# Routed expert tiles: rows turned by VectorE in 32-square pieces, first weights fetched per tile

## The chip, the cores and the metric

The kernel runs on one core of one Trainium2 chip. The metric is device time in microseconds (us) of one execution; lower is better. The engines of the core work from queues of their own: TensorE (PE, with its weight loads shown apart as PEld), VectorE (DVE), ScalarE (ACT), GpSimd (POOL) and SyncE (SP), which here only issues DMAs. A matmul on TensorE first loads a stationary operand[...] and then streams the moving operand past it; the sum lands in a PSUM bank of 512 fp32 columns.

## The reference

Everything is fp32. The input is x (2048 tokens by 256) and a context (1601 rows by 256). Four residual layers follow: a cross attention with 128 hidden columns, a mixture of experts, a two-way cross attention with a gate, and a small gated expert layer. The change is in the second one:

```python
def _ffn(x, w1, w2, w3):
    return jax.nn.silu(x @ w1.T) * (x @ w3.T) @ w2.T
shared = sum of _ffn over 2 shared experts, for every token
logits = xf @ router_w.T + expert_bias            # 8 routed experts
rw, sel = jax.lax.top_k(logits, 2)                # two experts for each token
rw = softmax(rw)
out = shared + sum over the two chosen experts of rw * _ffn(xf, w1[e], w2[e], w3[e])
```

An expert takes 256 columns to 512 hidden ones and back to 256.

## The kernel before

Tokens are held 128 to a tile, 16 tiles. The first attention (block 0) works in four blocks of 512 tokens. After it, `hT_f` has the normalised tokens turned (feature on the partition) and `h_f` has them as rows.

**Shared experts.** `hidden(e, b)` (L612) computes 512 tokens of the hidden layer of shared expert e: 16 fp32 matmuls with 512 moving columns, each of which shows as two instructions in the profile. `outward(e, b, act)` (L631) multiplies back and adds to the residual `xs`. Between the matmuls of the first two `hidden` calls stand the router's small matmuls (`route`, L605, one after each matmul).

**Routing.** From the router's result VectorE takes the best two experts (L647 to L682). Two small matmuls (L686) count the tokens of each expert that stand before a given one; from these VectorE computes the slot of each (token, choice) in a list sorted by expert, padded so that each tile of 128 slots belongs to one expert (L688 to L724): `owner[s]` is the expert of tile s, `used` the number of tiles. GpSimd then scatters the rows of `h_f` to the memory buffer `rows_in` by 32 indirect DMAs (L729), each of which waits for the one before. The rest of the shared experts' matmuls stand beside this on TensorE. Program order is: `hidden` for the first two blocks, `outward` for the first, first part of routing, `hidden` for the third, the counting matmuls, second part, scatters, and the remaining shared work.

**Routed tiles.** There are 39 possible tiles (`NSLOT`), and 36 of them (`NSURE`) are always run. `tiles(s0, s1, also)` (L841) is a software pipeline over them:

- `arrive(s)` (L792): one DMA on SP's queue brings 128 rows of 1 KB, two TensorE transposes turn them, VectorE copies the result to `rT`.
- `up(s, rT)` (L802): TensorE reads `owner[s]` into a register; `rT` is the stationary operand (128 tokens), the expert's first weights move with 512 columns, at an address from the register. Four matmuls, that is 8 instructions. Then silu on ScalarE and a product on VectorE give `act`, tokens on the partition.
- `turn(act)` (L817): four TensorE transposes and a ScalarE copy, to get `act` with the hidden index on the partition.
- `down(s, base, aT)` (L825): four matmuls (8 instructions) with 256 moving columns, a copy, and one indirect DMA on GpSimd's queue that scatters the rows to `rows_out`.

In round s of the loop TensorE does `up(s)`, `turn(s-1)`, the transposes of `arrive(s+2)`, `down(s-2)`. All three weights of all 8 experts lie in SBUF: L587 to L592 load them in 24 DMAs of 512 KB. `beside` (L856) issues the loads of the next layer in round 4 and reads `used` into a register on every engine in round 24. After the 36 tiles `ctx_rows("s", ks)` (L784) projects the context for the next layer (L231), and one branch on `used` (L867) runs tiles 36 to 38 or skips them; in this input it skips them.

The order on each engine's queue is made by a scheduler at build time, which may move an instruction past another that it does not depend on; `tc.issue_after` ties an order where it is used. SBUF is given out in pools; a load into a pool waits until the former user of the place is done, and everything behind it on SP's queue waits too.

Of the kernel before, what the change touches and what calls it, by code (L numbers as in the profile page):

```python
# [9 lines left out]
F32 = mybir.dt.float32  # L10
# [3 lines left out]
ALU = mybir.AluOpType  # L14
# [3 lines left out]
P = 128  # L18
S = 2048
SC = 1601  # L20
D = 256
DC = D // P
# [10 lines left out]
NE = 8  # L33
# [11 lines left out]
def xattn_ffn_kernel(ctx: ExitStack, tc: tile.TileContext, t: dict, out: bass.AP):  # L45
# [24 lines left out]

    def load_ctxT(pool, ends=(512, 1024, 1536, SC)):
        w = pool.tile([P, DC, SC], F32, name="ctxT")
        for lo, hi in zip((0,) + ends, ends):
            nc.sync.dma_start(w[:, :, lo:hi], t["ctxT"][:, :, lo:hi])
        return w

    rows_in = tc.dram_tile([NSLOT * P, D + 1], F32, name="rows_in")
    rows_out = tc.dram_tile([2 * S + P, D], F32, name="rows_out")  # L80

    rows_sub = tc.dram_tile([SC, 2 * D], F32, name="rows_sub")
# [31 lines left out]
    wk0 = load(cxp, "wk0", [P, DC, HID0], nc.scalar)  # L114
    ctxT = load_ctxT(cxp, (256, 512))
    load_x(0, nc.scalar)
# [25 lines left out]
    qkb = {n: load(raw, "b" + n, [P, DC]) for n in ("qc", "ks", "qs", "kc")}  # L142
    nc.sync.dma_start(wvs[:, :, 0:D], t["wvs"])

    make_identity(nc, ident)
# [187 lines left out]
    with ExitStack() as ph:  # L333
# [119 lines left out]
        for b in range(NB + 1):  # L453
# [3 lines left out]
            if b < NB:  # L457
# [3 lines left out]
                if last is not None:  # L461

                    add = sum_tiles(last[1], last[2], 0, NCT)
                    if b > 1:
                        tc.add_manual_dep(
                            add.ins, maxima[0].ins.name,
                            mybir.DependencyInfo(mybir.DependencyClass.Sync, mybir.DependencyReason.DATA),
                            reason="sums under the next maxima",
                        )
                    if b == 1:  # L470
                        with tc.issue_after(add.ins):
                            nc.gpsimd.memset(zero[:, 0:D], 0.0)
                            nc.gpsimd.iota(
                                zero[:, D : D + 1].bitcast(I32), pattern=[[0, 1]], base=2 * S, channel_multiplier=1
                            )
                        nc.sync.dma_start(
                            rows_in.rearrange("(n p) d -> p n d", p=P),
                            zero.unsqueeze(1).to_broadcast([P, NSLOT, D + 1]),
                        )
                acc = sp.tile([P, BW], F32, name="acc")  # L480

# [104 lines left out]
    rwp = sbuf(rx, "rwp")  # L586
    routed = []  # L587
    for n, src in enumerate(("ew1", "ew3", "ew2")):
        w = rwp.tile([P, NE, HID * DC], F32, name=f"r{src}")
        for e in range(NE):  # L590
            nc.sync.dma_start(w[:, e, :], t[src][NSH + e].rearrange("p c h -> p (c h)"))
        routed.append(w.rearrange("p e h -> p (e h)"))  # L592

    with ExitStack() as ph:
# [17 lines left out]
        def hidden(e, b):  # L612
            a1, a3, _ = experts[e]
            act = work.tile([P, NHC, BW], F32, name="act")
            for hc in range(NHC):
                cols = slice(hc * P, (hc + 1) * P)
                ps = [bank(ps_s) for _ in range(2)]
                for w, p in zip((a1, a3), ps):
                    for c in range(DC):
# [3 lines left out]
                        )  # L623
                        if routes:
                            routes.pop(0)()
# [5 lines left out]
        def outward(e, b, act):  # L631
            a2 = experts[e][2]
            for j in range(BT):
                i = b * BT + j
                y = bank(ps_m)[:, 0:D]
                for hc in range(NHC):
                    nc.tensor.matmul(  # L637
                        y, act[:, hc, j * P : (j + 1) * P], a2[:, hc, :], start=(hc == 0), stop=(hc == NHC - 1)
                    )
                nc.vector.tensor_tensor(xs[:, i, :], xs[:, i, :], y, ALU.add)  # L640

        shared = [(e, b) for e in range(NSH) for b in range(NB)]
        acts_of = {at: hidden(*at) for at in shared[:2]}
        outward(*shared[0], acts_of.pop(shared[0]))
        full = [P, NT, NE]
# [36 lines left out]
        nc.vector.tensor_tensor(both, hot[0], hot[1], ALU.add)  # L682
        acts_of[shared[2]] = hidden(*shared[2])
        at_ps = bank(ps_t)[:, : 2 * NE * NT].rearrange("p (k n) -> p k n", k=2)
# [57 lines left out]
        for n, at in enumerate(shared):  # L742
            if n > 1:
                if at not in acts_of:
                    acts_of[at] = hidden(*at)
                outward(*shared[n - 1], acts_of.pop(shared[n - 1]))
        outward(*shared[-1], acts_of.pop(shared[-1]))
    f0.close()
    ffw.close()


    l1 = ExitStack()
    l1k = sbuf(l1, "l1k", 1, "right")
    w1pool = sbuf(l1, "w1", 1, "right")
    w1 = {}
    raw1 = ExitStack()
    raw1p = sbuf(raw1, "raw1", 1, "right")
    bvs = []

    def second_layer_loads():  # L760
        bvs.append(load_row(l1k, "bvs", D))
        w1.update(
            ew=load(raw1p, "ew", [P, 2, DC, D]), ow=load(raw1p, "ow", [P, DC, D]), gw=load(raw1p, "gw", [P, DC, NE]),
            wv=load(raw1p, "wvc", [P, DC, D]), bg=load(raw1p, "bg", [P, DC]),
        )
        wg = t["wg"]
        w1["wg1"] = w1pool.tile([P, DC, D], F32, name="wg1")
        nc.sync.dma_start(w1["wg1"], wg[:, 0:DC, :])
        w1["wg2"] = raw1p.tile([P, DC, D], F32, name="wg2")
        nc.sync.dma_start(w1["wg2"], wg[:, DC : 2 * DC, :])  # L770
# [3 lines left out]
        w1["bv"] = load_row(raw1p, "bvc", D)  # L774
        return load_ctxT(raw1p)

    with ExitStack() as ph:
        work = sbuf(ph, "r0w", 3)
        in_tiled = rows_in.rearrange("(n p) d -> n p d", p=P)
        with nc.allow_non_contiguous_dma(reason="one element of each row"):  # L780
            nc.sync.dma_start(goes_to, rows_in.rearrange("(n p) d -> p n d", p=P)[:, :, D].bitcast(U32))


        def ctx_rows(n, r):  # L784
            project_T(
                ps_s, fold[n], ctxT, 0, SC,
                lambda o, cols, ps: nc.scalar.activation(
# [4 lines left out]
        def arrive(s):  # L792
            r = work.tile([P, D], F32, name="rin")
            nc.sync.dma_start(r, in_tiled[s][:, 0:D])
            tp = bank(ps_t)
            for c in range(DC):
                nc.tensor.transpose(tp[:, c * P : (c + 1) * P], r[:, c * P : (c + 1) * P], ident)
            rT = work.tile([P, DC, P], F32, name="rT")
            nc.vector.tensor_copy(rT.rearrange("p c q -> p (c q)"), tp[:, 0:D])
            return rT  # L800

        def up(s, rT):  # L802
            e = nc.tensor.value_load(owner[0:1, s : s + 1], min_val=0, max_val=NE - 1)
            base = nc.tensor.snap(e * (DC * HID))
            ps = [bank(ps_s) for _ in range(2)]
            for w, p in zip(routed, ps):
                for c in range(DC):
                    nc.tensor.matmul(  # L808
                        p, rT[:, c, :], w[:, bass.ds(base + c * HID, HID)], start=(c == 0), stop=(c == DC - 1)
                    )  # L810
            sl = work.tile([P, HID], F32, name="rsl")
            nc.scalar.activation(sl, ps[0], AF.Silu)  # L812
            act = work.tile([P, HID], F32, name="ract")
            nc.vector.tensor_tensor(act, sl, ps[1], ALU.mult)  # L814
            return base, act

        def turn(act):  # L817
            tp = bank(ps_t)
            for hc in range(NHC):
                nc.tensor.transpose(tp[:, hc * P : (hc + 1) * P], act[:, hc * P : (hc + 1) * P], ident)  # L820
            aT = work.tile([P, NHC, P], F32, name="raT")
            nc.scalar.copy(aT.rearrange("p c q -> p (c q)"), tp)
            return aT

        def down(s, base, aT):  # L825
            y = bank(ps_m)[:, 0:D]
            for hc in range(NHC):
                nc.tensor.matmul(  # L828
                    y, aT[:, hc, :], routed[2][:, bass.ds(base + hc * D, D)], start=(hc == 0), stop=(hc == NHC - 1)
                )  # L830
# [5 lines left out]
            )  # L836

        ks = l1k.tile([P, DC, SC], F32, name="ks")
        vs = l1k.tile([P, NCT, D + 1], F32, name="vs")
        kbs = l1k.tile([P, NCT], F32, name="kbs")  # L840
        def tiles(s0, s1, also):  # L841
            rT = {s: arrive(s) for s in range(s0, min(s0 + 2, s1))}
            hid, aTs = {}, {}
            for s in range(s0, s1 + 2):
                if s < s1:
                    hid[s] = up(s, rT.pop(s))
                if s0 <= s - 1 < s1:
                    base, act = hid[s - 1]
                    aTs[s - 1] = turn(act)
                if s + 2 < s1:  # L850
                    rT[s + 2] = arrive(s + 2)
                if s0 <= s - 2 < s1:
                    down(s - 2, hid.pop(s - 2)[0], aTs.pop(s - 2))
                also(s)

        def beside(s):  # L856
            nonlocal ctxT, count
            if s == 4:
                ctxT = second_layer_loads()
                nc.gpsimd.memset(vs[:, :, D : D + 1], 1.0)  # L860
            if s == 24:
                count = nc.values_load(used[0:1, 0:1], min_val=0, max_val=NSLOT)

        ctxT = count = None
        tiles(0, NSURE, beside)
        ctx_rows("s", ks)
        with tc.If(count > NSURE):  # L867
            tiles(NSURE, NSLOT, lambda s: None)
    rx.close()
# [429 lines left out]
```

## Time and profile before

| | us |
|---|---|
| median of 3 runs (lowest to highest) | 1075.43 (1075.1 to 1075.63) |
| the profiled execution's own time | 1075.38 |
| its span in the trace | 1073.6 |
| TensorE busy in the span | 1037.3 (97%) |
| routed tiles' matmuls: L808 / L828 | 131.2 / 68.0 |
| their transposes: L820 / L797 | 21.6 / 13.7 |
| granted TensorE clock, mean | 0.986 |

A group's row gives line, engine, operation, what is written and read, count, then busy time and the mean duration of one. Neighbouring matmuls overlap in the records[...], so the price of one in a stream is read from the distance of two starts, not from its duration. PEld rows are the weight loads that go with them. In a timeline or chain row the first number is the start, the second the length.

### The profile page before, as it was taken

What the parts mean: (1) busy time and instruction counts of PE and PEld (TensorE: products, weight loads), DVE (VectorE), ACT (ScalarE), POOL (GpSimd) and SP (SyncE); (2) the same over time, 40 slices, a digit from 0 to 9 for tenths busy, and PEclk for the clock granted to TensorE, in tenths of its full rate; (3) what the DMA queues carried; (4) which work ended last, traced back from release to release, by engine and by line L of the source; (5) the groups of instructions that cost most, each with busy time, mean ns of one, the idle gap of its engine ahead of it and who ended that gap; (6) DMA issues with size and microseconds to landing.
All of it is one profiled execution on the core that took longest, in us unless ns stands there. A gap on an engine that the chain in (4) does not pass through costs nothing.

```text
span 1073.6 us, 10976 instructions
## 1 busy us (share of the span) xinstructions
PE 1037.3 (97%) x3694; PEld 640.5 (60%) x3694; DVE 501.5 (47%) x1257; ACT 342.5 (32%) x569; POOL 234.5 (22%) x239
## 2 busy tenths in 40 slices
PE   7999999999999999999999999999999999999994
PEld 5644557655566566666665644464774476666872
DVE  4877785342222222222224745432504766676664
ACT  3765445111100112111114435322313633433321
POOL 2246450002232011111111007604044301110000
PEclk9999999999999999999999999999999999999996
DMA  9160004701113511111105000010004202110000
GB/s 318 61 159 0 1 1 159 312 5 40 35 49 58 158 45 45 47 48 45 40 26 162 6 1 0 1 40 20 20 20 141 80 1 60 40 49 10 11 10 20
DMA packets 42326, 62.81 MB, mean 59 GB/s; under 512 B 10461, under 2 KB 30045, under 8 KB 42270
## 3 DMA queue, kind: packets, MB, share of 16 engines
q1 hardware_dynamic: 35342, 43.73, 12.7%
q0 software_dynamic: 5824, 17.32, 5.1%
q10 hardware_dynamic: 1104, 1.05, 0.3%
q8 instruction: 31, 0.51, 0.2%
q14 instruction: 25, 0.20, 0.1%
HBM read 42.65 MB, written 19.44 MB: 58 GB/s over the span
## 4 chain that ended last, share of the span: by engine, by line
PE 84%; DVE 10%; ACT 2%; POOL 2%; issue 1%; DMA 1%; SPq 0%; DVEq 0%; ACTq 0%
PE sc L268 18%; PE sc L808 12%; PE sc L620 10%; PE mm L1022 8%; PE mm L828 6%; PE mm L637 5%; PE mm L327 4%; PE sc L231 3%; PE mm L518 2%; PE sc L1155 2%; PE sc L984 2%; DVE e L311 2%; PE tp L820 1%; POOL acc L448 1%; PE tp L1121 1%
## 5 line engine op out<-in xcount | busy, mean ns | idle before, releaser
L808 PE MATMUL sc<-rew,rT 128*128 x288 | 131.2, 599 | 0.8 <-DMA ew<-in_ew_dram 0.8
L620 PE MATMUL sc<-hT_f,ew 128*128 128x512 f32 x256 | 117.2, 600 | 0.0
L327 PE MATMUL mm<-vs,e 128*128 128x257 f32 (+1 forms) x416 | 96.4, 379 | 0.0
L311 DVE TENSOR_TENSOR e<-e,tp 128x2048 f32<-128x2048 f32 (+3 forms) x48 | 86.5, 1859 | 13.0 <-PE tp L303 13.0
L315 ACT ACTIVATE e<-e 128x2048 f32<-128x2048 f32 (+3 forms) x48 | 74.3, 1571 | 56.6 <-DVE e L311 56.1
L268 PE MATMUL sc<-hT,ks 128*128 128x512 f32 (+1 forms) x208 | 91.1, 592 | 0.0
L268 PE MATMUL sc<-qs,hT 128*128 128x512 f32 (+2 forms) x256 | 88.1, 500 | 0.9 <-ACT hT L963 0.9
L808 PEld LDWEIGHTS sc<-rew,rT 128*128 128x128 f32 x288 | 55.1, 192 | 55.5 <-issue 53.8
L1022 PE MATMUL mm<-e,hr 128*128 128x512 f32 (+2 forms) x256 | 88.0, 499 | 0.0
L270 ACT COPY e<-sc 128x512 f32<-128x512 f32 (+3 forms) x116 | 61.1, 535 | 81.0 <-PE sc L268 81.0
L276 DVE TENSOR_TENSOR m<-sc,m 128x512 f32<-128x512 f32 (+3 forms) x100 | 62.6, 626 | 51.5 <-ACT e L270 48.0
L327 PEld LDWEIGHTS mm<-vs,e 128*128 128x128 f32 (+1 forms) x416 | 77.2, 190 | 13.2 <-issue 2.8
L814 DVE TENSOR_TENSOR ract<-rsl,sc 128x512 f32<-128x512 f32 x36 | 24.8, 688 | 113.1 <-PE sc L808 113.1
L833 POOL DMA_INDIRECT rows_out<-rout,goes_to x36 | 35.0, 973 | 177.0 <-DVE rout L832 172.6
L620 PEld LDWEIGHTS sc<-hT_f,ew 128*128 128x128 f32 x256 | 46.4, 190 | 44.4 <-issue 44.0
L268 PEld LDWEIGHTS sc<-qs,hT 128*128 128x128 f32 x256 | 47.9, 189 | 37.2 <-issue 26.9
L1022 PEld LDWEIGHTS mm<-e,hr 128*128 128x128 f32 x256 | 48.2, 190 | 35.4 <-issue 28.2
L828 PE MATMUL mm<-rew,raT 128*128 x288 | 68.0, 379 | 0.0
L628 DVE TENSOR_TENSOR act<-sl,sc 128x512 f32<-128x512 f32 x32 | 22.0, 688 | 94.9 <-PE sc L620 91.7
L268 PEld LDWEIGHTS sc<-hT,ks 128*128 128x128 f32 (+1 forms) x208 | 38.3, 186 | 46.1 <-issue 44.0
L729 POOL DMA_INDIRECT rows_in<-h_f,slot x32 | 31.4, 982 | 143.4 <-DVE xs L640 75.0
L812 ACT ACTIVATE rsl<-sc 128x512 f32<-128x512 f32 x36 | 21.5, 597 | 125.8 <-PE sc L808 125.8
(267 smaller groups left out, 1466.8 us busy)
## 6 DMA issues: line engine op xcount, KB each, us to landing
rew<-in_ew_dram SPq DMA_DIRECT2D x24, 512.0 KB, 10.2
rows_in<-zero SPq DMA_DIRECT2D x1, 5011.5 KB, 20.7
rin<-rows_in SPq DMA_DIRECT2D x36, 128.0 KB, 2.1
g<-rows_out SPq DMA_DIRECT2D x8, 512.0 KB, 5.0
ew<-in_ew_dram SPq DMA_DIRECT2D x7, 512.0 KB, 5.5
rows_sub<-sgrow SPq DMA_DIRECT2D x12, 256.0 KB, 2.0
ctxT<-in_ctxT_dram SPq DMA_DIRECT2D x4, 512.0 KB, 7.1
out_dram<-xs SPq DMA_DIRECT2D x8, 256.0 KB, 2.1
```

The source lines that it names most:

```text
L268: nc.tensor.matmul(ps, kT[:, d, k * P : k * P + r], q[:, d, :], start=(d == 0), stop=(d == nd - 1))
L270: seen = [nc.scalar.copy(e[:r, k, :w], ps)]
L276: seen.append(nc.vector.tensor_tensor(m[:r, :w], ps, upto, ALU.max))
L311: nc.vector.tensor_tensor(part, part, bc[:r, :w].unsqueeze(1).to_broadcast([r, k1 - k0, w]), ALU.add)
L315: nc.scalar.activation(part, part, AF.Exp)
L327: nc.tensor.matmul(ov[:c, : D + 1], e[:r, k, j * P : j * P + c], v[:r, k, :], start=(k == 0), stop=(k == len(rows) - 1))
L620: nc.tensor.matmul(p, w[:, c, cols], hT[:, c, b * BW : (b + 1) * BW], start=(c == 0), stop=(c == DC - 1),)
L637: nc.tensor.matmul(y, act[:, hc, j * P : (j + 1) * P], a2[:, hc, :], start=(hc == 0), stop=(hc == NHC - 1))
L808: nc.tensor.matmul(p, rT[:, c, :], w[:, bass.ds(base + c * HID, HID)], start=(c == 0), stop=(c == DC - 1))
L828: nc.tensor.matmul(y, aT[:, hc, :], routed[2][:, bass.ds(base + hc * D, D)], start=(hc == 0), stop=(hc == NHC - 1))
L833: nc.gpsimd.indirect_dma_start(out=rows_out, out_offset=bass.IndirectOffsetOnAxis(ap=goes_to[:, s : s + 1], axis=0), in_=r, in_offset=None ...
L1022: nc.tensor.matmul(ov, hr[:, k, d * P : (d + 1) * P], e[:, k, :w], start=(k == 0), stop=(k == NT - 1))
```

## The change

- **A copy of the first weights in memory.** `first_w` is a new buffer of 8 x 1 MB. `reorder(e)` copies the two first weights of expert e into it with the feature index in another order, in 8 DMAs from memory to memory on SP's queue; 64 of them are issued during block 0, behind the clearing of `rows_in`. Only the last weight (`ew2`) of the routed experts is still loaded to SBUF as a whole.
- **Fetch per tile.** `fetch(s)` reads `owner[s]` on SP and brings that expert's 1 MB into one of three SBUF buffers.
- **Arrival by squares.** `arrive(s)` uses four DMAs with pieces of 256 bytes, and one VectorE transpose, which turns each 32 x 32 square by itself; the order of features that comes out is the one that `first_w` has. No TensorE transpose is left.
- **`up` with the operands changed round.** The weights are stationary (128 x 128), `rT` moves with 128 columns: 16 matmuls, 32 instructions. The result has the hidden index on the partition, so `turn` goes away and the product goes straight to `raT`. The loop is one stage shorter.
- **Routing earlier.** The router's matmuls all stand in the first `hidden` (one after each matmul, three in its second half); the first part of routing follows it, then the second `hidden`, the counting matmuls and the rest.
- **Start.** The fetches and arrivals of tiles 0 and 1 stand ahead of the last `outward`; the pools of the shared experts are closed after it.
- **Ties.** SP's fetches and arrivals, TensorE's register loads and VectorE's first turns are tied in order; the loads of the next layer go out one group a round from round 4 on.
- **Branches.** `ctx_rows` is cut in three pieces, and each of the tiles 36 to 38 has a branch of its own, one after each piece.

```diff
+    first_w = tc.dram_tile([NE, P, 2, DC, HID], F32, name="first_w")
+    def reorder(e):
+        for n, src in enumerate(("ew1", "ew3")):
+            for o in range(P // Q):
+                half = slice(o % DC * DC * Q, (o % DC + 1) * DC * Q)
+                nc.sync.dma_start(
+                    first_w[e, o * Q : (o + 1) * Q, n],
+                    t[src][NSH + e][half, o // DC, :].rearrange("(c q) h -> q c h", q=Q),
+                )
...
+                        for x in range(NE):
+                            reorder(x)
...
-    for n, src in enumerate(("ew1", "ew3", "ew2")):
-        w = rwp.tile([P, NE, HID * DC], F32, name=f"r{src}")
+    w = rwp.tile([P, NE, HID * DC], F32, name="rew2")
...
-                        if routes:
+                        for _ in range(min(len(routes), 3 if hc > 1 else 1)):
                             routes.pop(0)()
...
-        acts_of = {at: hidden(*at) for at in shared[:2]}
-        outward(*shared[0], acts_of.pop(shared[0]))
+        acts_of = {shared[0]: hidden(*shared[0])}
...
-        acts_of[shared[2]] = hidden(*shared[2])
+        acts_of[shared[1]] = hidden(*shared[1])
...
         def arrive(s):
-            r = work.tile([P, D], F32, name="rin")
-            nc.sync.dma_start(r, in_tiled[s][:, 0:D])
-            tp = bank(ps_t)
-            for c in range(DC):
-                nc.tensor.transpose(tp[:, c * P : (c + 1) * P], r[:, c * P : (c + 1) * P], ident)
+            r = work.tile([P, P // Q, DC, Q], F32, name="rin")
+            squares = in_tiled[s][:, 0:D].rearrange("(g a) (o w) -> o a g w", a=Q, o=P // Q)
+            for o in range(P // Q):
+                with behind("SP"):
+                    seen["SP"] = nc.sync.dma_start(r[o * Q : (o + 1) * Q].rearrange("a g c q -> a g (c q)"), squares[o])
             rT = work.tile([P, DC, P], F32, name="rT")
-            nc.vector.tensor_copy(rT.rearrange("p c q -> p (c q)"), tp[:, 0:D])
+            with behind("DVE"):
+                nc.vector.transpose(rT.rearrange("p c (g a) -> p g c a", a=Q), r)
...
+        def fetch(s):
+            w = wpool.tile([P, 2, DC, HID], F32, name="now")
+            with behind("SP"):
+                e = nc.sync.value_load(owner[0:1, s : s + 1], min_val=0, max_val=NE - 1)
+                e = nc.sync.snap(e)
+                seen["SP"] = nc.sync.dma_start(
+                    w.rearrange("p n c h -> p (n c h)"), first_w[bass.ds(e, 1)].rearrange("o p n c h -> p (o n c h)")
+                )
+            return w
...
-            for w, p in zip(routed, ps):
-                for c in range(DC):
-                    nc.tensor.matmul(
-                        p, rT[:, c, :], w[:, bass.ds(base + c * HID, HID)], start=(c == 0), stop=(c == DC - 1)
-                    )
+            for n, p in enumerate(ps):
+                for hc in range(NHC):
+                    for c in range(DC):
+                        mm = nc.tensor.matmul(
+                            p[:, hc * P : (hc + 1) * P], w[:, n, c, hc * P : (hc + 1) * P], rT[:, c, :],
+                            start=(c == 0), stop=(c == DC - 1),
+                        )
...
-        def turn(act):
...
+        def ahead(s):
+            fetched[s] = fetch(s)
+            rT[s] = arrive(s)
+
+        for s in range(2):
+            ahead(s)
+        outward(*shared[-1], acts_of.pop(shared[-1]))
...
+            for s in range(s0, s1 + 1):
                 if s < s1:
-                    hid[s] = up(s, rT.pop(s))
+                    hid[s] = up(s, rT.pop(s), fetched.pop(s))
+                if s + 2 < s1:
+                    ahead(s + 2)
                 if s0 <= s - 1 < s1:
-                    base, act = hid[s - 1]
-                    aTs[s - 1] = turn(act)
...
+                    down(s - 1, *hid.pop(s - 1))
                 also(s)
...
-        ctx_rows("s", ks)
-        with tc.If(count > NSURE):
-            tiles(NSURE, NSLOT, lambda s: None)
+        for n, s in enumerate(range(NSURE, NSLOT)):
+            ctx_rows("s", ks, n * 512, SC if s == NSLOT - 1 else (n + 1) * 512)
+            with tc.If(count > s):
+                tiles(s, s + 1, lambda s: None)
```

## The prediction

> **What bounds the kernel now.** I read the page first (shares, then the chain), then the chain around the routed tiles, then TensorE's timeline in one steady round and wherever short matmuls stand in a row, and last the DMA share of two stretches. From the page:
>
> ```profile
> PE 1037.3 (97%) x3694; PEld 640.5 (60%) x3694; DVE 501.5 (47%) x1257; ACT 342.5 (32%) x569; POOL 234.5 (22%) x239
> PE 84%; DVE 10%; ACT 2%; POOL 2%; issue 1%; DMA 1%; SPq 0%; DVEq 0%; ACTq 0%
> L808 PE MATMUL sc<-rew,rT 128*128 x288 | 131.2, 599 | 0.8 <-DMA ew<-in_ew_dram 0.8
> L820 PE MATMUL tp<-ident,ract 128*128 128x128 f32 x144 | 21.6, 273 | 0.0
> ```
>
> TensorE sets the time; in the routed tiles nearly nothing keeps it waiting (0.8 us ahead of L808, L820 never). So the change is priced by TensorE's stream there. The chain shows how the tiles begin, and two rounds:
>
> ```profile
> 334.01 8.65 PE mm L637 x40
> 342.65 1.31 SPq L68
> ...
> 346.17 4.85 DMA ew<-in_ew_dram
> ...
> 351.11 5.37 PE sc L808 x8
> ...
> 378.24 3.43 PE sc L808 x8
> 382.33 1.73 PE mm L828 x8
> 384.06 3.43 PE sc L808 x8
> ```
>
> L808 returns every 384.06 - 378.24 = 5.82 us. The first eight take 5.37 us in place of 3.43. The timeline of TensorE divides a round:
>
> ```profile
> 375.69 0.60 PE L820 MATMUL tp<-ident,ract 128*128 128x128 f32 x4
> 376.13 0.38 PE L797 MATMUL tp<-ident,rin 128*128 128x128 f32 x2
> 376.35 1.89 PE L828 MATMUL mm<-rew,raT 128*128 x8
> 378.07 3.60 PE L808 MATMUL sc<-rew,rT 128*128 x8
> 381.51 0.60 PE L820 MATMUL tp<-ident,ract 128*128 128x128 f32 x4
> ```
>
> By starts: four transposes 0.44, two 0.22, eight of L828 1.72, eight of L808 3.44 (0.430 each); sum 5.82, no gap. The shared experts' last matmul runs out at 347.8 (the timeline has L637 from 333.84 for 13.98) and the context projection begins at 561.9: 214.1 us for 36 tiles, of which 36 x 5.82 = 209.5 are rounds and 4.6 are the start (rows and pools late, then a first tile at about half pace).
>
> **The new `up`.** It has 32 pairs of weight load and matmul with 128 moving columns. Such pairs, real fp32 ones, stand in the trace:
>
> ```profile
> 230.20 0.38 PE L686 MATMUL tp<-both,before 128*128 128x128 f32 x2
> 230.42 0.39 PE L686 MATMUL tp<-both,ones 128*128 128x128 f32 x2
> 230.64 0.60 PE L637 MATMUL mm<-ew,act 128*128 128x256 f32 x2
> 572.18 0.86 PEld L231 LDWEIGHTS sc<-ctxT,fold_s 128*128 128x128 f32 x7 [0.24 <-issue]
> ```
>
> Starts of L686 are 0.22 us apart for two: 0.11 each. Seven weight loads in a row (65 moving columns) take 0.86, the last 0.19 long: (0.86 - 0.19) / 6 = 0.112. The weight load sets this pace[...]. The upper bound is the value projection of block 0 (L244, 18 pairs in a row, first start to last end 2.46 us, the last 0.27 long): (2.46 - 0.27) / 17 = 0.129. There the stream has two holes in which a PSUM bank is awaited; in `up` both banks were freed a round ago. I take 0.1117: 32 x 0.1117 = 3.57 us in place of 3.44.
>
> A rule speaks against it. The Trainium skill, "TensorE: Matmul & The Clock Gate", section "Back-to-back issue gap", gives sustained load-and-matmul pairs as about 81 ns with 128 columns and 131 ns with 512, a ratio of 0.62. Cutting 512 columns in four would then cost 4 x 0.62 = 2.5 times: `up` 8.5 us, a round 10.2, and the kernel some 155 us slower. This trace has 0.112 against 0.430, a ratio of 0.26. I use the trace.
>
> **The round after.** Six transposes go (-0.66), `up` gains 0.13, `down` keeps 1.73: 3.57 + 1.73 = 5.30 us, 36 x 5.30 = 190.8, a gain of 18.7. For this the other parts must stay under 5.30 us a tile:
> - VectorE: the old copy (0.42) becomes a transpose of 256 columns. The trace has none; between that 0.42 and the 0.69 of a 512-column product (L814). I take 0.5. VectorE was busy 43.4 of 174 us, 1.5 a tile; without that cover each 0.1 would be 3.6 us in all.
> - ScalarE loses a copy of 0.59. The product that `down(s-1)` needs is done about 1.1 us after `up(s-1)`, and `down(s-2)` (1.73) stands between, in the last round too.
> - TensorE's register load stays (0.30 us on its sequencer, which runs ahead); four address computations a tile go.
> - SP: a register load (0.30 on TensorE, 0.47 on SP at L862), about 0.2 of register work, five DMAs. These cost 0.32 (L794) to 0.43 (L62), and 1.0 when queues are full (24 loads in 23.89 us at L591). So 2.1 to 5.7 us; I take 2.8. The fetch of tile s+2 waits for `up(s-1)`; the four row DMAs and the next layer's loads wait behind it, and VectorE's turn for them, two rounds ahead of need.
> - DMA: each tile fetches 1.05 MB. The stretches:
>
> ```profile
> 176.00:206.00 30.00, 29.97 (x118) 16.93 (x117) 5.59 (x13) 6.90 (x13) 0.00 (x0) 1.00 0.99 388
> 376.00:550.00 174.00, 174.00 (x659) 109.15 (x658) 43.38 (x90) 35.50 (x60) 29.18 (x30) 1.00 0.14 44
> ```
>
> (The last two columns are the share of the 16 DMA engines and GB/s.) While weights streamed at 388 GB/s TensorE kept its pace. At that rate 1.05 MB takes 2.7 us; rows and scatters had 0.14 of 5.82 = 0.8 us, and 256-byte pieces can hardly double it (4,992 pieces of 4 bytes at L781 landed in 4.6 us). About 3.8 of 5.30 us. One 512 KB load on an empty queue landed in 4.2 us, so 1 MB takes about 5.6; the buffers give it two rounds, over 10. The scatter's landing (2.4 us, plus 0.97 issue) has 5.3.
>
> Against this stands the skill's "DMA: Bandwidth & Descriptors", table in section "Bandwidth": 1 MB alone is given 6.15 us. If fetches went one by one at that pace they would set the round: see the rivals. I take the 388 GB/s, from loads of the same kind.
>
> **The start.** Router matmuls: 64 pairs, 0.11 us each wherever they stand; moved, not saved. `hidden` of the first block then ends near 175.7 + 13.7 + 7.1 = 196.5 and the second near 210.2; the first part of routing (5.5 us on VectorE, with three residual adds in it) fits under it. The counting matmuls come at 210 in place of 230.2, the scatters end 20 us earlier, near 321 in place of 340.8. The last `outward` runs from 340.9 to 347.8 as now, so the rows, 1 MB and the turns of tiles 0 and 1 are there: the 4.6 us go. The cover is 20 us; when it is gone, the turns, which stand ahead of the last adds on VectorE, hold those up too.
>
> **Hidden parts.** The 64 copies go out on SP behind the clearing at 50.2, at 0.33 to 1.0 us each (21 to 64 us), with 8.4 MB read and written, about 67 us at the 125 GB/s that the clearing's stretch moved. SP has nothing else until 175.4, and the data is wanted at 320. Without that gap the 8 remaining weight loads would be late. Sixteen loads of 512 KB go from a stretch in which TensorE did not wait: nothing.
>
> **Branches.** Two more. At the present one TensorE waits 0.45 us and the first matmul is stretched: the last weight loads end at 573.0, the next matmul starts at 573.62. I take 0.7 each; between 0.45 and 1.3 (the chain's hole there). Cost 1.4.
>
> **Sum** against the profiled execution: -18.7 - 4.6 + 1.4 = -21.9: span 1073.6 to 1051.7, time 1075.38 to 1053.5. The median shown, 1075.43, differs by 0.05, so the same number stands for it.
>
> **Rivals.**
> 1. *The start stays* (the scatters do not end earlier, or something else on SP is late): 1053.5 + 4.6 = 1058. For: each scatter waits for the last one's landing, and fetches now share the DMA engines. Against: 20 us of slack.
> 2. *The pairs run at 0.129*: round 5.86, 36 x 5.86 = 211, gain 214.1 - 211 - 1.4 = 1.7, time 1074. For: the L244 row. Against: its holes are bank waits.
> 3. *The fetch sets the round, and it gets slower.* Place: SP's queue and the DMA engines in the tiles. With 1 MB in 6.15 us (170 GB/s), 1.05 + 0.13 MB are 6.9 us a tile, 36 x 6.9 = 249, time 1075.4 + 249 + 1.4 - 214.1 = 1112. It decides from (214.1 - 1.4) / 36 = 5.91 us a tile on, 200 GB/s; SP's upper bound of 5.7 comes near. Against: 388 GB/s, with nothing in flight but such loads.
>
> **How the numbers follow.** The sum as it stands 0.72 (own range 1049 to 1058: branches, a microsecond or two of changed order in later stages), rival 1 0.10, rival 2 0.07, rival 3 0.11. The range leaves out rivals 2 and 3 (0.18) and is 1047 to 1066, with room for a round of up to 5.5 us. What a measurement can tell from no change is about 0.2%, 2.2 us. Faster: 0.72 + 0.10 + half of rival 2 = 0.85; same 0.04; slower 0.11.
>
> **What will show it.** In the profile after: `up` starts every 5.30 us; 32 of its matmuls 0.112 apart; no PE tp rows in the tiles; fetches landing in under 7 us and never a releaser of `up`; no hole between L637 and the first `up`; three holes of 0.7 us at the branches. It is wrong if `up` shows idle time ended by DMA or VectorE, if pairs are further apart, or if a stage outside the tiles has moved.

## The result, and the profile after

The changed kernel takes 1107.84 us (1105.28 to 1108.18), the kernel before, measured beside it, 1076.02 us: a ratio of 1.0288, 95% interval 1.0272 to 1.0304. The prediction was 1053.5 us, about 22 us faster; what came is some 32 us slower. The span grew from 1073.6 to 1106.1 us.

Three parts of the page of the changed kernel (shares, TensorE's busy tenths in 40 slices, groups of instructions):

```profile
PE 1031.2 (93%) x4342; PEld 694.6 (63%) x4342; DVE 502.9 (45%) x1257; ACT 321.4 (29%) x533; POOL 235.7 (21%) x239
...
PE   7999999999999987788889999999999999999994
...
L840 PE MATMUL sc<-rT,now 128*128 128x128 f32 x1152 | 135.8, 276 | 16.4 <-issue 15.6
...
L855 PE MATMUL mm<-rew,raT 128*128 x288 | 70.9, 390 | 23.7 <-DVE raT L849 23.7
```

L840 is the new `up`, L855 is `down`. TensorE's busy time fell by 6 us and the span grew by 32, so the loss is waiting: 16.4 us ahead of `up` and 23.7 ahead of `down`, where the routed tiles before had 0.8 us ahead of their matmuls and 1.8 ahead of their transposes. The slices put it into one place, the 7s and 8s from 387 to 581 us, the tiles. (The chain of waits, from which the prediction started, is of no use here: on this trace it stops at a branch, at 606.60 us, and never reaches the tiles.)

TensorE's timeline of the changed kernel (start, length, what, count), first where the tiles begin, then in a later round:

```profile
334.94 13.98 PE L645 MATMUL mm<-ew,act 128*128 128x256 f32 x64
348.76 7.31 PE L840 MATMUL sc<-rT,now 128*128 128x128 f32 x64
355.90 1.89 PE L855 MATMUL mm<-rew,raT 128*128 x8
357.63 3.73 PE L840 MATMUL sc<-rT,now 128*128 128x128 f32 x32
361.20 1.89 PE L855 MATMUL mm<-rew,raT 128*128 x8
362.93 3.73 PE L840 MATMUL sc<-rT,now 128*128 128x128 f32 x32
```

```profile
447.44 3.81 PE L840 MATMUL sc<-rT,now 128*128 128x128 f32 x32 [0.92 <-issue]
452.10 1.99 PE L855 MATMUL mm<-rew,raT 128*128 x8 [0.85 <-DVE raT L849]
455.00 3.81 PE L840 MATMUL sc<-rT,now 128*128 128x128 f32 x32 [0.92 <-issue]
459.66 1.99 PE L855 MATMUL mm<-rew,raT 128*128 x8 [0.85 <-DVE raT L849]
461.49 3.73 PE L840 MATMUL sc<-rT,now 128*128 128x128 f32 x32
466.08 1.99 PE L855 MATMUL mm<-rew,raT 128*128 x8 [0.85 <-DVE raT L849]
468.99 1.24 PE L840 MATMUL sc<-rT,now 128*128 128x128 f32 x9 [0.92 <-issue]
```

The first fence is the prediction come true. The last shared matmul (L645, start 334.94 for 13.98) runs straight into the first `up`, with no hole; the round is 362.93 - 357.63 = 5.30 us; `up` takes 361.20 - 357.63 = 3.57, so its pairs are 0.1116 apart; `down` takes 1.73. It holds for the tiles 1 to 6. In the second fence the same work takes 455.00 - 447.44 = 7.56, then 461.49 - 455.00 = 6.49 and 468.99 - 461.49 = 7.50 us. `down` starts 4.6 us after `up` in place of 3.57 (1.02 to 1.09 of waiting for the product raT) in each of them. `up` starts 2.9 after `down` in place of 1.73 (about 1.18 of waiting) in every round up to tile 16, and in every other one after it. From tile 6 to tile 35 the mean round is (587.34 - 378.83) / 29 = 7.19 us. That is 29 x (7.19 - 5.30) = 54.8 us: the prediction missed the time by 1107.84 - 1053.5 = 54.3.

Which `down` stands there shows on VectorE, whose timeline in the same stretch of the changed kernel is:

```profile
454.13 0.42 DVE L859 COPY rout<-mm 128x256 f32<-128x256 f32 x1 [2.09 <-PE mm L855]
454.47 0.43 DVE L812 STREAM_TRANSPOSE rT<-rin 128x256 f32<-128x256 f32 x1
458.92 0.69 DVE L849 TENSOR_TENSOR raT<-rsl,sc 128x512 f32<-128x512 f32 x1 [4.02 <-PE sc L840]
459.53 0.44 DVE L812 STREAM_TRANSPOSE rT<-rin 128x256 f32<-128x256 f32 x1
461.69 0.42 DVE L859 COPY rout<-mm 128x256 f32<-128x256 f32 x1 [1.73 <-PE mm L855]
```

The product that the `down` at 459.66 waits for (L849, 458.92 for 0.69) is that of the `up` of 455.00. So up to tile 6 TensorE has `up(s+1)` between `up(s)` and `down(s)`; after it `down(s)` comes right behind `up(s)`, with nothing in between that could cover silu and product. And on VectorE the turn (L812, 454.47) that the next `up` (455.00) needs stands behind a copy of an output (L859, 454.13) that waits for `down`. The profile names nothing that ended most of these waits of `up` (`issue`); in one round, at 409.57, it names the turn (0.87 us), and in the one shown the turn ends at 454.90, 0.1 before `up` starts. Run 6 below tests the reading. The rows which that turn takes had been asked for 18 us earlier, at 436.6 (the four row DMAs of tile 16; in run 5 below such a DMA lands 5.1 us after its issue, the median between 376 and 400 us), so it was not late data that held it. Nothing in the kernel orders the turn against the copy, or `down(s)` against `up(s+1)`; the build has placed them so. The Trainium skill, "PSUM — Partial Sum Buffer", section "Engine vs sequencer instructions", calls VectorE's queue strictly first in, first out, and has TensorE's matmuls start in program order; the trace agrees: the turn, its data long asked for, starts within 0.4 us of the copy in front of it.

The last fence of the changed kernel answers the DMA share shown before (the columns are those of the windows there, the last two the DMA share and GB/s):

```profile
176.00:206.00 30.00, 29.96 (x129) 17.80 (x129) 10.67 (x73) 9.89 (x18) 0.00 (x0) 1.00 0.38 141
376.00:550.00 174.00, 141.22 (x993) 126.50 (x991) 36.27 (x74) 15.61 (x27) 25.47 (x28) 1.00 0.63 204
```

The first row is no longer the stream of weights at 388 GB/s, since sixteen of these loads went. In the second, the tiles, the DMA engines are busy 0.63 of the time, at 204 GB/s. That is near the 200 GB/s at which rival 3 (the fetch sets the round) begins to decide, and its forecast, 1112 us, is only 4 us from the measurement. Two stories, then: the order of two queues (theory A in what follows), or the fetched megabyte in one form or another (theory B). The first runs were chosen to part them.

### The profile page after: what moved, and what is told of

It is laid out like the page before. It is cut to its first block, busy times and chain, and to the rows that moved or that the text cites. A ratio compares the mean times of both kernels' runs of the same rounds, so it can differ in the third digit from the quotient of the medians.

```text
span 1106.1 us, 12495 instructions
## 1 busy us (share of the span) xinstructions
PE 1031.2 (93%) x4342; PEld 694.6 (63%) x4342; DVE 502.9 (45%) x1257; ACT 321.4 (29%) x533; POOL 235.7 (21%) x239
## 5 line engine op out<-in xcount | busy, mean ns | idle before, releaser
L840 PE MATMUL sc<-rT,now 128*128 128x128 f32 x1152 | 135.8, 276 | 16.4 <-issue 15.6
L840 PEld LDWEIGHTS sc<-rT,now 128*128 128x128 f32 x1152 | 132.6, 192 | 24.2 <-issue 21.9
L628 PE MATMUL sc<-hT_f,ew 128*128 128x512 f32 x256 | 114.1, 595 | 0.0
L855 PE MATMUL mm<-rew,raT 128*128 x288 | 70.9, 390 | 23.7 <-DVE raT L849 23.7
L335 PEld LDWEIGHTS mm<-vs,e 128*128 128x128 f32 (+1 forms) x416 | 77.5, 191 | 13.3 <-issue 2.8
L849 DVE TENSOR_TENSOR raT<-rsl,sc 128x512 f32<-128x512 f32 x36 | 24.7, 687 | 129.6 <-PE sc L840 129.6
L855 PEld LDWEIGHTS mm<-rew,raT 128*128 128x128 f32 x288 | 51.9, 190 | 35.5 <-DVE raT L849 29.9
```

The lines of the kernel that those rows point to most:

```text
L335: nc.tensor.matmul(ov[:c, : D + 1], e[:r, k, j * P : j * P + c], v[:r, k, :], start=(k == 0), stop=(k == len(rows) - 1))
L628: nc.tensor.matmul(p, w[:, c, cols], hT[:, c, b * BW : (b + 1) * BW], start=(c == 0), stop=(c == DC - 1),)
L840: mm = nc.tensor.matmul(p[:, hc * P : (hc + 1) * P], w[:, n, c, hc * P : (hc + 1) * P], rT[:, c, :], start=(c == 0), stop=(c == DC - 1),)
L849: nc.vector.tensor_tensor(aT.rearrange("p c q -> p (c q)"), sl, ps[1], ALU.mult)
L855: nc.tensor.matmul(y, aT[:, hc, :], second_w[:, bass.ds(base + hc * D, D)], start=(hc == 0), stop=(hc == NHC - 1))
```

## The experiments

All are measured against the kernel before on the same chip. It took 1079.29 us beside the first four and 1073.22 beside the last four, so between the two groups, and with the changed kernel, ratios and rounds compare better than times.

**1. A tie on TensorE.** `down` stays behind the latest `up` that was issued before it, which is `up(s+1)`:

```diff
+            seen["up"] = mm
...
             for hc in range(NHC):
+              with behind("up"):
                 nc.tensor.matmul(
                     y, aT[:, hc, :], second_w[:, bass.ds(base + hc * D, D)], start=(hc == 0), stop=(hc == NHC - 1)
```

> The changed kernel, with one more tie: each tile's last product (down of tile s-1) is queued on TensorE behind the last matmul of up of tile s. Nothing else. Theory A (order): the chip could always have run a round in 5.30 us, and lost 54 us because from tile 6 on the queue has down(s) directly behind up(s), so that TensorE waits for the product, and VectorE's turn of the next rows stands behind a copy that waits for down. With the tie every round is 5.30 us, the tiles take 36 x 5.30 = 191 us in place of 245, and the time is 1052 to 1056 us. Theory B (fetch): 1 MB a tile cannot come faster, the order only follows it. Then up waits for its weights instead, a round stays at 6.5 to 7 us and the time at 1095 to 1108 us.

Measured: 1085.82 us (1082.8 to 1088.76), ratio 1.0067 (1.0041 to 1.0092). Neither value came. A part of the loss went, and what was left had one shape in every round. The timeline of this kernel, TensorE and VectorE (L857 is `down`, L861 the copy of the output):

```profile
449.98 3.81 PE L840 MATMUL sc<-rT,now 128*128 128x128 f32 x32 [0.92 <-issue]
...
453.63 1.89 PE L857 MATMUL mm<-rew,raT 128*128 x8
...
455.56 0.43 DVE L861 COPY rout<-mm 128x256 f32<-128x256 f32 x1 [0.62 <-PE mm L857]
455.90 0.43 DVE L812 STREAM_TRANSPOSE rT<-rin 128x256 f32<-128x256 f32 x1
...
456.44 3.81 PE L840 MATMUL sc<-rT,now 128*128 128x128 f32 x32 [0.92 <-issue]
```

`down` now follows `up` without waiting. But the turn still stands behind the copy, the copy waits for `down`, and `up` waits for the turn: 456.44 - 453.63 = 2.81 from `down` to the next `up` in place of 1.73. The round is 6.46 us, 29 x 1.16 = 34 us in all. There are two orders that matter, not one: the expectation had named both, but took it that the tie on TensorE would put the second right too.

**2. Half the fetch.** Only the first of the two first weights is fetched, and used for both products; no tie:

```diff
-            w = wpool.tile([P, 2, DC, HID], F32, name="now")
+            w = wpool.tile([P, DC, HID], F32, name="now")
...
-                    w.rearrange("p n c h -> p (n c h)"), first_w[bass.ds(e, 1)].rearrange("o p n c h -> p (o n c h)")
+                    w.rearrange("p c h -> p (c h)"), first_w[bass.ds(e, 1), :, 0].rearrange("o p c h -> p (o c h)")
...
-                            p[:, hc * P : (hc + 1) * P], w[:, n, c, hc * P : (hc + 1) * P], rT[:, c, :],
+                            p[:, hc * P : (hc + 1) * P], w[:, c, hc * P : (hc + 1) * P], rT[:, c, :],
```

> The changed kernel with no further tie; only the first of the two first weights is fetched (512 KB a tile) and stands in for the second too, so the routed result is not the reference's. The build gives this kernel the program's order in the tiles (up(s), down(s-1)) to the end. Theory A: 1052 to 1056 us, as with the tie, because the order is right. Theory B: the same, because half the data is well under a round. It shows that the size of the fetch is what the build's order hangs on; the next kernel parts the theories.

Measured: 1057.29 us (1056.92 to 1067.05), ratio 0.9834 (0.9778 to 0.9889). Taken alone this would have made theory B look right: halve the transfer and the loss is gone. But another thing changed with it. With buffers of half the size the queues as built have `up(s+1)` ahead of `down(s)` through to the last tiles. Only from tile 12 to 14 does a part of `down(s)` come early, which costs 1.1 us in all; in the other rounds nothing waits in TensorE's timeline:

```profile
453.07 3.73 PE L840 MATMUL sc<-rT,now 128*128 128x128 f32 x32
456.64 1.89 PE L855 MATMUL mm<-rew,raT 128*128 x8
458.37 3.73 PE L840 MATMUL sc<-rT,now 128*128 128x128 f32 x32
```

So the run doesn't part the two by itself, and the next one was needed.

**3. Half the fetch, in the changed kernel's order.** As 2, with `down(s)` put right behind `up(s)` from tile 6 on in the program, and each later `up` tied behind the `down` before it:

```diff
+                      with behind("down" if s >= 7 else "none"):
...
-                nc.tensor.matmul(
+                seen["down"] = nc.tensor.matmul(
...
+                late = s >= 7 and s0 <= s - 1 < s1
+                if late:
+                    down(s - 1, *hid.pop(s - 1))
                 if s < s1:
                     hid[s] = up(s, rT.pop(s), fetched.pop(s))
...
-                if s0 <= s - 1 < s1:
+                if not late and s0 <= s - 1 < s1:
                     down(s - 1, *hid.pop(s - 1))
```

> As half_fetch (512 KB a tile, the second first weight left out), but from tile 6 on TensorE is given the changed kernel's order: down(s) directly behind up(s), up(s+1) behind it. VectorE turns the rows of the next tile ahead of the copy that follows down. Theory A: TensorE waits about 1.1 us a round for the product, a round is 6.4 us from tile 7 on (29 rounds), time about 1054 + 29 x 1.1 = 1086 us. Theory B: with half the data nothing waits, 1052 to 1057 us.

Measured: 1084.34 us, ratio 1.0055 (1.0035 to 1.0076). TensorE's timeline (L841 is `up`, L856 `down`) has the wait for the product back, and a round of 391.00 - 384.58 = 6.42 us:

```profile
384.58 3.73 PE L841 MATMUL sc<-rT,now 128*128 128x128 f32 x32
389.17 1.99 PE L856 MATMUL mm<-rew,raT 128*128 x8 [0.85 <-DVE raT L850]
391.00 3.73 PE L841 MATMUL sc<-rT,now 128*128 128x128 f32 x32
```

With the same half megabyte the order on TensorE alone costs 27 us. The fetch can't be charged with that.

**4. Twice the fetch.** Both ties (the second is that of run 5), and a second megabyte a tile into two buffers that nobody reads:

```diff
+            more = morepool.tile([P, 2, DC, HID], F32, name="more")
+            with behind("SP"):
+                seen["SP"] = nc.sync.dma_start(
+                    more.rearrange("p n c h -> p (n c h)"), first_w[bass.ds(e, 1)].rearrange("o p n c h -> p (o n c h)")
+                )
```

> The kernel with the tie, and each tile fetches a second megabyte that nobody reads; VectorE's copy after down is tied behind the turn of the rows two tiles on. It measures the room on the DMA engines. In the changed kernel a tile keeps the 16 engines busy for about 4.05 us (0.58 of a mean round of 6.97). Theory A: a second megabyte adds 2.7 to 3.2 us, about 7 us, over the 5.30 of TensorE: a round of about 7 us, time 1054 + 36 x 1.7 = 1110 to 1120 us. Theory B (1 MB already needs 6.5 to 7 us): two need 11 to 13 us, time 1260 to 1330 us.

Measured: 1103.98 us, ratio 1.0238 (1.0201 to 1.0275). Its window, and a turn on VectorE:

```profile
400.00:560.00 160.00, 135.43 (x952) 123.38 (x951) 34.08 (x71) 14.81 (x25) 22.28 (x24) 0.97 1.03 363
...
493.03 0.45 DVE L813 STREAM_TRANSPOSE rT<-rin 128x256 f32<-128x256 f32 x1 [1.28 <-DMA rin<-rows_in]
```

Here DMA is the bound: a share of 1.03 at 363 GB/s, the turn that `up` needs waits for its rows to land, the mean round is (583.99 - 385.49) / 29 = 6.84 us, and the time is somewhat under what either theory gave. Three of these rounds hold an `up` of 5.27 to 6.75 us in place of 3.81, in stretches where the granted clock fell to 0.87 to 0.89; from tile 17 on, without such, the round is 6.45. So two megabytes and the rows (2.10 + 0.13 MB) need 6.5 to 6.8 us, and one (1.18 MB) an estimated 3.4 to 3.6 at the same rate. The prediction's 3.8 us of DMA per tile was about right, and one megabyte has room in a round of 5.30.

**5. Both ties.** Experiment 1's tie, and on VectorE the copy of an output behind the turn of the tile two ahead:

```diff
-                nc.vector.transpose(rT.rearrange("p c (g a) -> p g c a", a=Q), r)
+                seen["turn", s] = nc.vector.transpose(rT.rearrange("p c (g a) -> p g c a", a=Q), r)
...
-            nc.vector.tensor_copy(r, y)
+            with behind(("turn", s + 2)):
+                nc.vector.tensor_copy(r, y)
```

> The changed kernel with two ties more, nothing left out: the matmuls of down(s) stay behind the last matmul of up(s) in TensorE's queue (which, as the tiles go, puts them behind up(s+1) for every s), and VectorE's copy of a tile's output, rout(s), stays behind the turn of s+2. Theory A (the whole error of the prediction is the order in two queues): the round is 5.30 us in all 36 tiles, no hole ahead of up, and the kernel takes what the prediction's sum said with the branch as predicted, 1052 to 1056 us, some 20 to 25 us below the kernel before. Theory B (with fetches of a megabyte the round has another floor, DMA or the load on SBUF, that half the fetch hid): the round stays above 5.8 us and the kernel above 1070 us, with DMA busy over 0.85 of the stretch.

Measured: 1054.51 us (1054.3 to 1054.86), ratio 0.9823 (0.9809 to 0.9836). All of the change is in it, with the full fetch; only the order of two queues differs from the changed kernel, and it is 53 us faster than that (by the ratios 4.6%, some 50 us). Page, a window (the same columns as above), and both engines in one round:

```profile
PE 1016.9 (97%) x4342; PEld 691.9 (66%) x4342; DVE 502.5 (48%) x1257; ACT 321.2 (31%) x533; POOL 235.6 (22%) x239
...
L840 PE MATMUL sc<-rT,now 128*128 128x128 f32 x1152 | 134.3, 275 | 0.0
...
L857 PE MATMUL mm<-rew,raT 128*128 x288 | 68.0, 379 | 0.0
```

```profile
400.00:560.00 160.00, 159.10 (x1102) 143.16 (x1101) 45.84 (x104) 22.26 (x37) 29.28 (x32) 1.00 0.69 229
```

```profile
453.93 3.73 PE L840 MATMUL sc<-rT,now 128*128 128x128 f32 x32
457.50 1.89 PE L857 MATMUL mm<-rew,raT 128*128 x8
457.77 0.69 DVE L850 TENSOR_TENSOR raT<-rsl,sc 128x512 f32<-128x512 f32 x1 [3.22 <-PE sc L840]
458.37 0.44 DVE L812 STREAM_TRANSPOSE rT<-rin 128x256 f32<-128x256 f32 x1
459.23 3.73 PE L840 MATMUL sc<-rT,now 128*128 128x128 f32 x32
459.43 0.42 DVE L862 COPY rout<-mm 128x256 f32<-128x256 f32 x1 [0.61 <-PE mm L857]
```

Idle time of 0.0 ahead of both groups, a round of 459.23 - 453.93 = 5.30 us, and the DMA engines carry more per microsecond than in the slow kernel (229 against 195 GB/s in the same window), because the rounds are shorter. VectorE's turn (458.37) now comes ahead of the copy (459.43), a round early. A fetch lands 5.2 us after its issue. Theory B had 1070 us and over.

**6. The tie on VectorE alone.** Run 5's second edit, without run 1's:

```diff
+            with behind(("turn", s + 2)):
+                nc.vector.tensor_copy(r, y)
```

> The changed kernel with VectorE's tie alone: rout(s) behind the turn of s+2, TensorE's queue as the program builder leaves it, so that from tile 6 on down(s) stands directly behind up(s). Theory A (two orders, each with its own price): up(s+1) no longer waits for a turn, but TensorE waits for silu and product of its own tile, the 0.85 to 1.04 us of the changed kernel's rounds, in every round: about 6.3 to 6.4 us from tile 6 on, some 1053 + 29 x 1.05 = 1083 us (1080 to 1088). Theory B (either tie is enough, since one chain runs through both): 1052 to 1060 us. Theory C (VectorE's order was only a consequence of TensorE's): as the changed kernel, 1100 to 1110 us.

Measured: 1086.36 us, ratio 1.0119 (1.0103 to 1.0134). In its timeline `up` follows `down` without a wait and `down` waits for its own product in each round of 461.57 - 455.15 = 6.42 us:

```profile
455.15 1.99 PE L855 MATMUL mm<-rew,raT 128*128 x8 [1.20 <-DVE raT L849]
456.98 3.73 PE L840 MATMUL sc<-rT,now 128*128 128x128 f32 x32
461.57 1.99 PE L855 MATMUL mm<-rew,raT 128*128 x8 [0.85 <-DVE raT L849]
```

With 1, 5 and 6 the two orders have a price each:

| | time, us (ratio) | round, us, tiles 12 to 35 | `down` waits for its product | `up` waits for a turn |
|---|---|---|---|---|
| changed kernel | 1107.84 (1.0288) | 7.07 | each round | each, from tile 16 every other |
| tie on TensorE | 1085.82 (1.0067) | 6.45 | no | each round |
| tie on VectorE | 1086.36 (1.0119) | 6.43 | each round | no |
| both | 1054.51 (0.9823) | 5.31 | no | no |

The last column but one and the last are read from the idle time noted in the timelines. The rounds add up. The late turn alone costs 6.45 - 5.30 = 1.15 us a round and the late product alone 6.42 - 5.30 = 1.12; where the changed kernel has both in one round it takes 7.56, which is 2.26 over 5.30, against 2.27 for the sum of the two. From tile 16 on two of its rounds hold twice the wait of `down` (1.09 and 1.02 over its 3.57), once the late turn (1.18 over 1.73) and once 0.10 of a stretched `down`: (1.09 + 1.02 + 1.18 + 0.10) / 2 = 1.70 us a round, and 7.00 is the mean of the 6.49 and 7.50 shown. With one tie only one wait is left, but in every round.

**7. One branch in place of three.** As 5, with the table loads in one piece and tiles 36 to 38 under one branch:

```diff
-        for n, s in enumerate(range(NSURE, NSLOT)):
-            ctx_rows("s", ks, n * 512, SC if s == NSLOT - 1 else (n + 1) * 512)
-            with tc.If(count > s):
-                tiles(s, s + 1, lambda s: None)
-            seen.clear()
+        ctx_rows("s", ks)
+        with tc.If(count > NSURE):
+            tiles(NSURE, NSLOT, lambda s: None)
+        seen.clear()
```

> Both ties, and the last three tiles under one branch again with one set of table loads, as in the kernel before. The prediction priced two branches more at 0.7 us each. If a branch that isn't taken costs what the holes of the changed kernel's end show (0.54 us each), this one is about 1.1 us below the kernel with both ties; if the holes are hidden by the scatters behind, the two are within 0.3 us.

Measured: 1053.12 us (1050.83 to 1053.67), ratio 0.9806 (0.9793 to 0.9819): 1.4 us less than with three, though the intervals of the two ratios overlap. It has the lowest median of the study, 20 us below the kernel before. The context projection (L239) with three branches and the first matmul behind it (L969), in TensorE's timeline of run 5, and the same two ends with one branch, in that of run 7:

```profile
540.45 3.60 PE L239 MATMUL sc<-ctxT,fold_s 128*128 128x512 f32 x8
544.35 2.81 PE L239 MATMUL sc<-ctxT,fold_s 128*128 128x512 f32 x6 [0.30 <-PEq L917]
547.46 5.37 PE L239 MATMUL sc<-ctxT,fold_s 128*128 128x512 f32 x18 [0.30 <-PEq L917]
...
575.69 1.89 PE L969 MATMUL mm<-wg,vT 128*128 128x256 f32 x8
```

```profile
540.23 11.30 PE L239 MATMUL sc<-ctxT,fold_s 128*128 128x512 f32 x32
...
574.61 1.89 PE L968 MATMUL mm<-wg,vT 128*128 128x256 f32 x8
```

The idle time noted is 0.30 us, but the price is more. Six L239 matmuls at 0.43 are 2.58, and from one hole to the next there are 547.46 - 544.35 = 3.11: 0.53 a branch. The whole stretch, with the same matmuls in it, takes 575.69 - 540.45 = 35.24 us with three branches and 574.61 - 540.23 = 34.38 with one: two more cost 0.86 us there. The rest of the difference between the two times stands elsewhere in the traces and is not explained.

**8. Five buffers.** The changed kernel with more room for fetches:

```diff
-        wpool = sbuf(ph, "r0x", 3)
+        wpool = sbuf(ph, "r0x", 5)
```

> The changed kernel with five buffers for the fetched weights instead of three and no tie more. In the order as built the down that comes directly behind its own up appears at tile 12 instead of tile 6. Theory A (order sets the time): six rounds more of about 5.3 us instead of 7.0 us, about 10 us below the changed kernel: 1096 to 1099 us. Theory B (the fetch's arrival or its waiting for a buffer sets the round): with two buffers more the fetches run further ahead and most of the loss goes, below 1075 us.

Measured: 1095.12 us (1092.4 to 1104.37), ratio 1.022 (1.0176 to 1.0264), just under what theory A gave. The fetches do run ahead (tile 14's is issued 27 us before its `up`, where the changed kernel has 19), and it helps no tile by itself: rounds are as long as before, 7.07 us from tile 12 on. What changed is where the order slips. Half of `down(11)` comes ahead of `up(12)`, and all of `down(12)` right behind it:

```profile
408.67 2.76 PE L855 MATMUL mm<-rew,raT 128*128 x12
411.48 3.81 PE L840 MATMUL sc<-rT,now 128*128 128x128 f32 x32
415.12 3.01 PE L855 MATMUL mm<-rew,raT 128*128 x12
```

In the changed kernel this came at tile 6. `up(12)` starts at 411.48 in place of 424.74, 13.3 us earlier, and that is the gain (12.6 us between the spans; 0.7% between the ratios).

## Why the prediction was wrong

**The local sums held.** Both the step for `up` (0.1117 a pair, 3.57 us) and the step for the round (5.30) are in the trace to the second decimal, in the first tiles of the changed kernel and in all of run 5. The rule of the Trainium skill ("TensorE: Matmul & The Clock Gate", section "Back-to-back issue gap") that would have made `up` 2.5 times as long was rightly set aside: 0.1116 against 0.430 us is again a ratio of 0.26, not 0.62. So rival 2 is out. The turn takes 0.435 us where I took 0.5. The counting matmuls came at 210.66 (forecast 210) and the first `up` without a hole, so the start's 4.6 us did go, and rival 1 is out. Branches: 1.4 us were forecast for two more. Runs 5 and 7 differ by that much in their medians, but the traces show 0.86 at the branches, so 0.7 each was too much and the agreement of the medians is luck.

**The step that failed** is in "The round after": "The product that `down(s-1)` needs is done about 1.1 us after `up(s-1)`, and `down(s-2)` (1.73) stands between", together with VectorE's turn being "two rounds ahead of need". Both read the order of the loop as the order of the queues, and so put two waits at nothing. They are true of the loop, and in the queues of TensorE and VectorE nothing held them. From tile 6 on no other tile's work stood between `up(s)` and `down(s)`, which costs 1.12 us a round, and turns stood behind copies that waited for `down`, which costs 1.15 in each round that has it. The prediction listed VectorE's 1.5 us of work a tile as cover and never asked, for the rounds, what stood in front of the turn on that queue. Run 5 puts both orders right and takes 1054.51 us.

**Rival 3 was right on the sign and near on the number, and wrong on the cause.** It had 1112 us, from a round of 6.9 us set by the fetch; the round was 7.19. In run 5 the fetch is whole and the round 5.30; in run 3 the fetch is halved and the round 6.42. The 1 MB in 6.15 us of the Trainium skill ("DMA: Bandwidth & Descriptors", section "Bandwidth") doesn't bind either: here a fetch of this size lands 5.2 us after its issue, and fetches follow each other every 5.30. The row was a weak ground for the rival anyway. It is for transfers that GpSimd issues, while these go out on SP's queue, and it gives 341 GB/s beside the 6.15 us, where the prediction worked out 170. That rival 3 came within 4 us is luck, and a forecast that agrees with a time is no proof of its mechanism: it took half the fetch in the wrong order (run 3) and the whole fetch in the right one (run 5) to part the two.

**What of the forecast gain is missing even in order.** By spans run 5 gained 1073.6 - 1052.7 = 20.9 us where 21.9 were forecast. The tiles went from 214.1 to 540.45 - 347.72 = 192.7 us, 1.9 more than the sum's 190.8; one round of 7.12 us holds 12 transposes of the next layer's weights (L957), which stood behind the tiles before. What follows the tiles went from 511.7 to 512.3, though these transposes (1.8 us) had left it. The branches' 0.9 makes up for half of that; the other 1.5 us are not explained. Against the kernel before on its own chip the gain is 1073.22 - 1054.51 = 18.7 us. The traces compared above come from different chips, so 18.7 is the better measured of the two.

**Open.** Why the build's order changes at tile 6 was not seen; what the runs show is that it moves with the size of the fetched buffer and with the number of buffers (runs 2 and 8). `up` with the operands changed round but weights kept in SBUF was not tried, so what the fetch costs by itself is only bounded: runs 2 and 5 have the same round of 5.30 us, and their ratios overlap (0.9778 to 0.9889 and 0.9809 to 0.9836).

## What to carry to other kernels

A sum over a software pipeline holds only if the order in each queue is the order of the loop: for each instruction that waits, ask what stands in front of it on its own engine, and tie the order where an edge that the sum rests on is not a data dependency. When a resource is changed and the time follows, look whether the order of the queues changed with it: half the fetch was as fast as run 5 because of the order that came along with it. A steady state is read some ten rounds in; here the first six were as forecast.

## What the hardware showed that was not expected

Fetches of 1 MB every 5.30 us, with rows and scatters beside them, kept the DMA engines busy 0.69 of the time and TensorE showed no idle time for them (run 5); with 2 MB a tile they ran at 363 GB/s and TensorE waited. A hole in TensorE's stream costs more than the idle time noted for it. The two rounds of the changed kernel from 455.00 to 468.99 take 3.39 us over 2 x 5.30, and their three holes are noted with 0.85 + 0.85 + 0.92 = 2.62: about 0.26 more for each. Part of it is that work after a hole is longer (8 of L855 show 1.99 us after a wait against 1.89 without), part that without a hole the records overlap (`up` is noted with 3.73 us, and `down` starts 3.57 after it). So the 40 us of idle on the page stand for most of the 55 lost.
